# The last stage of a convolution-attention-experts kernel: another fixed order, a drain of GpSimd's queue put elsewhere, bias rows in two loads

## The chip, the cores and the metric

One core of one Trainium2 chip runs the whole kernel in one launch. The metric is the device time of an execution in microseconds. Times below are from the kernel before; start times count from the start of the profiled span.

## What is computed

Eight images of 56 x 56 tokens with 128 channels pass a deformable convolution layer (layer 0), then attention, then an expert layer, all in f32. Only the expert layer matters here:

```python
logits = einsum('bsd,ed->bse', x, gate_w) + gate_b      # x: 8 x 3136 x 128, 64 experts
probs = softmax(logits, axis=1)                          # over the tokens of an image
vals, idx = top_k(probs.transpose(0, 2, 1), 8)           # 8 tokens for each expert and image
pooled = einsum('bked,bke->bed', x[idx], vals)           # one row for each expert and image
h = gelu(concat(pooled, 1) @ weight1)                    # 129 x 512 for each expert
out = concat(h, 1) @ weight2                             # 513 x 128; its last row is the bias
outputs.at[idx].add(out * vals)                          # added to the chosen tokens
```

The result is x + outputs. A token can be chosen by several experts, so an addition in place must not lose any of them.

## The kernel before, in words

Up to some 2540 us the kernel runs convolution, attention and the gate of the experts, interleaved by a list of steps (ORDER) that is fixed in the source. In its last steps it also lays ready the slots: a slot is one of the K = 8 tokens of an expert in an image. `slot_f` holds the slots' token numbers, `slot_c` their weights. What the change touches comes after that: the block `with tc.manual_schedule` at L1974 to L2038, where each engine executes its instructions in the order in which the text writes them, and the call of `store` behind it.

**Names.** The images are in two groups, g = 0 (images 0 to 3) and g = 1 (4 to 7); the 64 experts in two halves, h = 0 and h = 1. So a 128-partition tile holds one group and one half: 4 images x 32 experts. The two layers of the experts are computed in four quarters q of 16 experts: quarters 0 and 1 are half 0, quarters 2 and 3 half 1.

**A quarter.** `hidden(q)` (L1806, 32 matmuls on PE) multiplies by weight1; `unload` copies the result to SBUF (ACT); `turned(q)` transposes it (PE, L1821), adds the bias (DVE, L1822) and applies gelu (ACT, L1827); `outputs(q)` (PE, L1835, 128 small matmuls, then a copy on ACT, L1842) multiplies by weight2; `gathered(q)` transposes (PE, L1847) and files the result in `outT` (DVE, L1849).

**A total.** Several slots can name the same token. For each slot of (g, h), the kernel computes the sum of what all slots of the same token in the same group, in halves h2 <= h, give. `share` (L1584, L1597) builds the weight of expert to slot, in 8 products and 7 additions on DVE for each (g, h, h2); `steps(last, n)` issues n of these pieces. `expand(g, h, h2)` (L1856) spreads such a share over the 4 images into a `wide` tile: for h = 0 with one DVE multiplication (L1860), for h = 1 with four ACT operations (L1870). `totals(g, h, h2)` multiplies `wide` by the experts' outputs `oe` (PE, L1915, 16 matmuls); where h2 = h, it first transposes `outT` (L1906) and adds the bias rows `b2` (DVE, L1909), and at its end adds the sums to the tokens' rows (DVE, L1924, two additions). These rows are in `rows` for g = 0 and `low` for g = 1, gathered from DRAM by POOL's indirect DMAs.

**Repeated slots.** Only one slot of each token may write its row. For g = 1, `first_only(1, h)` marks the others: `again` (DVE, L1883) from `wide` (g, h, h), 16 matmuls in one column each (two passes of 8, L1893, `pc`), `at` and `once` (DVE, L1895 and L1896). A marked slot's row number is put beyond the end, and the store leaves it out.

**The store.** `store(g, h)` (L1953 to L1972) issues 8 indirect DMAs on POOL (L1959), each writing 128 rows of 512 B to the output. The four calls are (0,0), (1,0), (0,1), (1,1). Ahead of half 1 POOL waits for half 0's writes to have landed (`done_`), since rows may be the same tokens; behind (1,0) stands a `drain` of GpSimd (L1972); behind (1,1) a wait for all writes.

**What sets order.** On each engine, the text's order. `gen` is a ring of five PSUM banks that the transposes, `hidden`, `pc` and `pf` share (L282). `freed` hands out SBUF buffers of used weights to `came` (later weight loads on SP), `base`, `expand` and `first_only`, in the order of the calls. SP issues the weight loads (512 KB each) and the loads of `b2` in one queue.

Of the kernel before, what the change touches and what calls it, by code (L numbers as in the profile page):

```python
# [17 lines left out]
C = 128  # L18
# [15 lines left out]
DH = 512  # L34
# [211 lines left out]
def local_kernel(ctx, tc, a, pos, out, flag):  # L246

    nc = tc.nc
# [1485 lines left out]
    w1, w2 = a["L1_ffn_weight1"], a["L1_ffn_weight2"]  # L1734
# [8 lines left out]
    def second_weights(e, pool, tag, bufs):  # L1743

        t = pool.tile([P, EG, 4, C], F32, tag=tag, name=f"w2t{e}", bufs=bufs)
        nc.sync.dma_start(
            t.rearrange("p e f o -> p e (f o)"),
            w2[e : e + EG, :DH, :].rearrange("e (p f) o -> p e (f o)", f=4),
        )
        for k in range(EG):  # L1750
            experts["second", e + k] = t[:, k]
# [50 lines left out]
    def hidden(q):  # L1802
        ph = gen(f"eph{q}")
        for r in range(4):
            for j in range(4):
                nc.tensor.matmul(  # L1806
                    ph[32 * j : 32 * (j + 1), :],
                    pps[q % 2][:, r, j, :],
                    experts["first", EB * q + 4 * r + j],
                    start=r == 0,  # L1810
                    stop=r == 3,
                )
        return ph

    def unload(ph):
        nc.scalar.copy(eh, ph.rearrange("r (h f) -> r f h", f=4))
# [27 lines left out]
    def gathered(q):  # L1844
        pt = gen(f"eot{q}")
        for r in range(4):
            nc.tensor.transpose(pt[:, r * P : (r + 1) * P], eo[:, r, :], ident)  # L1847
        e0 = EB * (q % 2)
        nc.vector.tensor_copy(  # L1849
            outT[:, q // 2, :, e0 : e0 + EB].rearrange("o b e -> o e b"),  # L1850
            pt.rearrange("o (e b) -> o e b", e=EB)[:, :, :NB],
        )
# [3 lines left out]
    def expand(g, h, h2):  # L1856
        pool, tag, n = next(freed)
        wide = pool.tile([P, K, 4, 32], F32, tag=tag, name=f"wide{g}{h}{h2}", bufs=n)
        if h == 0:
            nc.vector.tensor_mul(  # L1860
                wide,
                shares[g, h, h2].unsqueeze(2).to_broadcast([P, K, 4, 32]),
                experts["same"]
                .rearrange("p (b e) -> p b e", b=4)
                .unsqueeze(1)
                .to_broadcast([P, K, 4, 32]),
            )
        else:
            for b in range(4):
                nc.scalar.activation(  # L1870
                    wide[:, :, b],
                    shares[g, h, h2],
                    AF.Copy,
                    scale=experts["same"][:, 32 * b : 32 * b + 1],
                )
        wides[g, h, h2] = wide

    def first_only(g, h):

        pool, tag, n = next(freed)  # L1880
        again = pool.tile([P, K, P], F32, tag=tag, name=f"again{g}{h}", bufs=n)
        wides[g, h] = again
        nc.vector.scalar_tensor_tensor(  # L1883
            again,
            wides[g, h, h].rearrange("p k b e -> p k (b e)"),
            0.0,
            experts["upper"].unsqueeze(1).to_broadcast([P, K, P]),
            op0=ALU.is_gt,
            op1=ALU.mult,
        )  # L1890
        pc = gen(f"pc{g}{h}")
        for k in range(K):
            nc.tensor.matmul(pc[:, k : k + 1], again[:, k], unit, start=True, stop=True)  # L1893
        at = experts["pool"].tile([P, 2, K], F32, tag="twice", name=f"at{g}{h}")[:, 0]
        nc.vector.tensor_scalar_add(at, slot_f[:, g, h], float(4 * g * T))  # L1895
        nc.vector.scalar_tensor_tensor(  # L1896
            experts["once", g, h], pc[:, :K], float(NB * T), at, op0=ALU.mult, op1=ALU.add
        )
# [3 lines left out]
    def totals(g, h, h2):  # L1902

        if h2 == h:
            pt = gen(f"pt_o{g}{h}")
            nc.tensor.transpose(  # L1906
                pt[:, :P], outT[:, h, 4 * g : 4 * g + 4, :].rearrange("o b e -> o (b e)"), ident
            )
            nc.vector.tensor_add(oes[g, h], pt[:, :P], b2[:, h])  # L1909
        for k0 in range(0, K, 4):  # L1910
            if h2 == 0:
                pfs[g, h, k0] = gen(f"pf{g}{h}_{k0}")
            pf = pfs[g, h, k0]
            for k in range(4):
                nc.tensor.matmul(  # L1915
                    pf[:, k * C : (k + 1) * C],
                    wides[g, h, h2][:, k0 + k].rearrange("p b e -> p (b e)"),
                    oes[g, h2],
                    start=h2 == 0 and k == 0,
                    stop=h2 == h and k == 3,  # L1920
                )
            if h2 == h:
                r = rows[g, h][:, k0 : k0 + 4].rearrange("p k c -> p (k c)")
                nc.vector.tensor_add(r, r, pf)  # L1924

    def steps(line, n):

        for _ in range(n):
            got = next(line, None)
            while got is not None and got.when and not got.us:  # L1930
                got = next(line, None)

    def came(which, n):
        load, todo = (first_weights, second_weights)[which], left[which]
        for _ in range(min(n, len(todo))):
            load(todo.pop(0), *next(freed))
# [16 lines left out]
    def store(g, h):  # L1953
        for k0 in range(0, K, 4):
            with tc.tile_critical(no_gpsimd_drain=True):
                if h and not g and not k0:
                    nc.gpsimd.wait_ge(done_, 16 * 2 * K)
                for k in range(k0, k0 + 4):
                    nc.gpsimd.indirect_dma_start(  # L1959
                        out=every,  # L1960
                        out_offset=bass.IndirectOffsetOnAxis(
                            ap=experts["once", g, h][:, k : k + 1], axis=0
                        ),
                        in_=rows[g, h][:, k, :],
                        in_offset=None,
                        bounds_check=NB * T - 1,
                        oob_is_err=False,
                    ).then_inc(done_, 16)
                if h and g and k0:
                    nc.gpsimd.wait_ge(done_, 16 * 4 * K)  # L1970
                elif g and k0:
                    nc.gpsimd.drain()  # L1972

    with tc.manual_schedule(engines=engines):  # L1974
        for k, at in enumerate(first_at):
            first_weights(EFIRST + EG * k, *at)
        for k, at in enumerate(second_at):
            second_weights(EFIRST + EG * k, *at)
        for pp in pps:
            nc.gpsimd.memset(pp.rearrange("p r j e -> p (r j e)"), 0.0)  # L1980
        pos_ = [ps.tile([P, 512], F32, tag=t, name=f"epo_{t}") for t in ("held", "av")]
        for t in pos_:
            nc.vector.memset(t, 0.0)
        widen(0)
        widen(1)
        steps(slots(NB // 2 - 1), 9)
        last = share(1)
        steps(last, 3)
        unload(hidden(0))
        for h in range(2):  # L1990
            for _ in base(1, h):
                pass
        steps(last, 1)
        ph = hidden(1)
        came(0, 9)
        b2 = fin.tile([P, 2, C], F32, tag="b2", name="b2")
        for h in range(2):
            for q in range(4):
                nc.sync.dma_start(b2[32 * q : 32 * q + 32, h], w2[32 * h : 32 * h + 32, DH, :])
        came(0, 2)  # L2000
        widen(2)
        steps(last, 9)
        turned(0)
        unload(ph)
        widen(3)
        steps(last, 6)
        for g in range(2):
            expand(g, 0, 0)
        outputs(0)
        turned(1)  # L2010
        first_only(1, 0)
        came(1, 8)
        gathered(0)
        outputs(1)
        came(1, 4)
        unload(hidden(2))
        steps(last, 15)
        gathered(1)
        for g in range(2):
            totals(g, 0, 0)  # L2020
        turned(2)
        ph = hidden(3)
        unload(ph)
        expand(0, 1, 0)
        expand(1, 1, 0)
        steps(last, 99)
        outputs(2)
        turned(3)
        for g in range(2):
            totals(g, 1, 0)  # L2030
        gathered(2)
        for g in range(2):
            expand(g, 1, 1)
        first_only(1, 1)
        outputs(3)
        gathered(3)
        for g in range(2):
            totals(g, 1, 1)  # L2038
    for h in range(2):
        for g in range(2):  # L2040
            store(g, h)
# [813 lines left out]
```

## Time and profile before

| | |
|---|---|
| median of 3 runs | 2654.75 us (2653.42 to 2655.34) |
| the profiled execution's own time | 2656.84 us |
| its span | 2655.0 us |
| granted TensorE clock, mean | 0.972 |
| busy: PE, DVE, ACT, POOL | 93%, 82%, 73%, 82% |
| the experts' stage | about 2540 to 2626 us, then the stores of half 1 |
| POOL's stores, half 0 | 2595.48 to 2616.39 us, 16 DMAs |
| drain L1972 | 2608.04 to 2623.66 us |
| POOL's stores, half 1 | 2626.60 to 2646.89 us, 16 DMAs |

In the profile, PE is TensorE, PEld its weight loads, DVE VectorE, ACT ScalarE, POOL GpSimd, SP the engine that issues most loads. "POOLq" is POOL's instruction sequencer; it takes drains, waits and moves, and goes ahead of the engine behind it. In a timeline each line has start, duration, engine, source line, operation and operands; the bracket holds the engine's idle time before it and what ended that. In a table of windows each engine's busy time in a stretch stands with its count of instructions, and PEclk is the granted clock.

### The profile page before, as it was taken

The page shows a single profiled execution, that of the slowest core. Times are in us where ns is not written, and L with a number is a line of the kernel's source. Part 1 is how long each engine was busy: PE and PEld are TensorE (multiplying, and loading weights), DVE is VectorE, ACT ScalarE, POOL GpSimd, SP SyncE. Part 2 cuts the span into 40 slices and gives each one's busy share as a digit, 9 for nine tenths or more (in the row PEclk, how much of TensorE's full clock was granted, in tenths as well). Part 3 has the DMA queues.
Part 4 walks back from the last instruction along what each step waited for, and adds up shares of the span by engine and source line. Part 5 has one row for each costly group of instructions (what it writes and reads, how often), then busy time and mean ns, then how long its engine had stood idle before and what let it go on. Part 6 is the DMA issues. An engine that isn't in the chain of part 4 may idle for free. (4 is left out here: it accounts for less than half of the span.)

```text
span 2655.0 us, 47647 instructions
## 1 busy us (share of the span) xinstructions
PE 2472.8 (93%) x16297; PEld 1887.9 (71%) x16297; DVE 2164.0 (82%) x4659; ACT 1948.4 (73%) x4532; POOL 2180.2 (82%) x2315
## 2 busy tenths in 40 slices
PE   3799999999999999999999899999999999999974
PEld 3677877777776778777776667767777777777743
DVE  6888877899898987888889897888889988865662
ACT  2356787888787887888778677977888887876631
POOL 3686889889998899989899899987998899882244
PEclk8799999999999999999999999999999999999987
DMA  5665544544554454545454354544465445325083
GB/s 159 204 214 205 208 163 161 198 128 158 189 190 125 160 194 173 175 150 167 169 183 151 122 198 170 181 149 148 162 201 171 145 166 192 136 88 197 23 276 119
DMA packets 274416, 442.63 MB, mean 167 GB/s; under 512 B 14452, under 2 KB 127476, under 8 KB 274164
## 3 DMA queue, kind: packets, MB, share of 16 engines
q1 hardware_dynamic: 184340, 382.09, 41.4%
q10 hardware_dynamic: 86464, 50.94, 6.3%
q0 software_dynamic: 3360, 6.45, 0.8%
q8 instruction: 132, 2.16, 0.4%
q14 instruction: 120, 0.98, 0.1%
HBM read 386.04 MB, written 53.48 MB: 166 GB/s over the span
## 5 line engine op out<-in xcount | busy, mean ns | idle before, releaser
L732 POOL TENSOR_TENSOR g<-g 128x128 f32<-128x128 f32 (+6 forms) x1075 | 1420.9, 1331 | 105.6 <-DVE g L715 25.4
L715 DVE TENSOR_TENSOR g<-g,tp 128x3200 f32<-128x3200 f32 (+1 forms) x200 | 695.0, 3477 | 18.3 <-ACT tp L706 15.9
L1203 PEld LDWEIGHTS av<-v,pe 128*128 128x128 f32 (+2 forms) x5200 | 627.6, 188 | 97.3 <-issue 60.9
L1203 PE MATMUL av<-v,pe 128*128 128x129 f32 (+2 forms) x5200 | 682.7, 277 | 2.8 <-ACT pe L1173 1.6
L1066 PE MATMUL sc<-zT,qT 128*128 128x384 f32 (+8 forms) x1622 | 656.9, 516 | 17.1 <-DVE S L1092 9.9
L1092 DVE TENSOR_SCALAR_CACHE_REDUCE S<-sc 128x512 f32<-128x512 f32 (+5 forms) x783 | 443.3, 576 | 210.1 <-PE sc L1066 124.7
L1140 ACT ACTIVATE S<-S,low 128x512 f32<-128x512 f32 (+5 forms) x783 | 478.8, 638 | 41.9 <-DVE low L1108 30.1
L1173 ACT COPY pe<-tr 128x512 f32<-128x512 f32 (+3 forms) x775 | 380.2, 501 | 144.2 <-PE tr L1158 110.5
L1158 PE MATMUL tr<-ident,S 128*128 128x128 f32 x2516 | 392.3, 276 | 12.6 <-DVE S L1092 9.5
L1158 PEld LDWEIGHTS tr<-ident,S 128*128 128x128 f32 x2516 | 297.0, 142 | 130.7 <-issue 67.0
L1066 PEld LDWEIGHTS sc<-zT,qT 128*128 128x128 f32 (+1 forms) x1622 | 246.6, 187 | 114.1 <-issue 43.3
L576 DVE SCALAR_TENSOR_TENSOR pv<-xg,dw,pv 128x448 f32<-128x448 f32 x448 | 305.7, 682 | 14.2 <-ACT pv L573 8.4
L877 PEld LDWEIGHTS pm<-fc,hid 128*128 128x128 f32 x1600 | 200.4, 193 | 37.6 <-issue 22.6
L877 PE MATMUL pm<-fc,hid 128*128 128x128 f32 x1600 | 222.2, 282 | 1.8 <-POOL hid L862 1.3
L856 PE MATMUL ph<-xT,fc 128*128 128x512 f32 (+2 forms) x448 | 207.3, 551 | 5.2 <-DVE xT L803 3.2
L863 ACT ACTIVATE hid<-ph,b_fc 128x512 f32<-128x512 f32 (+2 forms) x224 | 140.8, 634 | 95.8 <-PE ph L856 92.8
L667 POOL TENSOR_TENSOR taps<-taps,a 128x252 f32<-128x252 f32 (+1 forms) x288 | 191.9, 666 | 8.8
L657 POOL TENSOR_TENSOR a<-w 128x756 f32<-128x756 f32 (+1 forms) x96 | 136.5, 1422 | 20.9 <-DVE w L648 18.4
L760 ACT COPY ys<-ptg 128x128 f32<-128x128 f32 (+1 forms) x200 | 52.6, 263 | 89.4 <-PE ptg L749 47.5
L1140 ACT ACT_TABLE_LOAD x87 | 111.6, 1283 | 4.6 <-DVE pv L576 2.3
L749 PE MATMUL ptg<-ident,g 128*128 128x128 f32 (+1 forms) x650 | 92.0, 307 | 21.7 <-POOL g L732 21.6
L749 PEld LDWEIGHTS ptg<-ident,g 128*128 128x128 f32 (+1 forms) x650 | 88.6, 221 | 25.5 <-POOL g L732 23.7
(328 smaller groups left out, 3712.8 us busy)
## 6 DMA issues: line engine op xcount, KB each, us to landing
g<-img SPq DMA_DIRECT2D x192, 1600.0 KB
w1t<-in_L_ffn_weight_dram SPq DMA_DIRECT2D x32, 512.0 KB
w2t<-in_L_ffn_weight_dram SPq DMA_DIRECT2D x32, 512.0 KB
xin<-in_x_dram SPq DMA_DIRECT2D x56, 224.0 KB
xTd<-xc ACTq DMA_DIRECT2D x56, 224.0 KB
img<-st ACTq DMA_DIRECT2D x112, 112.0 KB
out_dram<-t ACTq DMA_DIRECT2D x24, 448.0 KB
g<-img SPq DMA_DIRECT2D x8, 800.0 KB
```

What stands on the lines that cost most here:

```text
L576: nc.vector.scalar_tensor_tensor(p3, src, dw[:, k : k + 1], p3, op0=ALU.mult, op1=ALU.add)
L667: nc.gpsimd.tensor_add(dst, dst, a5[:, :nt, kx])
L715: nc.vector.tensor_mul(g3, g3, tp[:n, lt % 4].unsqueeze(2).to_broadcast([n, NTAP * NG, 32]))
L732: nc.gpsimd.tensor_add(g[:n, o * C : (o + w) * C], g[:n, o * C : (o + w) * C], g[:n, i * C : (i + w) * C])
L856: nc.tensor.matmul(ph[:, :n], fc1[:, f * P : (f + 1) * P], xT[:, :n], start=True, stop=True)
L877: nc.tensor.matmul(four(pm, m)[:, i, :], h[:, i * P : (i + 1) * P], fc2[:, f, :], start=False, stop=i == m - 1 and f == 3,)
L1066: nc.tensor.matmul(pp[h * HALF : h * HALF + qw, c0 : c0 + m], qT[:, q0 : q0 + qw], zTs[b, g][:, k0 : k0 + m], start=True, stop=not seg.las ...
L1092: nc.vector.tensor_scalar(S[p0:p1, c0:c1], pp[p0:p1, c0:c1], -SCALE, None, ALU.mult, ALU.min, accum_out=(mn[p0:p1, i, j + k : j + k + 1] i ...
L1140: nc.scalar.activation(S[p0:p1, c0:c1], S[p0:p1, c0:c1], AF.Exp, bias=low[p0:p1, i : i + 1], scale=-1.0)
L1158: nc.tensor.transpose(pt[:m, k + p0 : k + w], S[p0:w, k : k + m], ident[p0:w, p0:w])
L1173: nc.scalar.copy(pe[:, : full * P], pt[:, : full * P])
L1203: nc.tensor.matmul(p3[h * HALF : h * HALF + qw, i % 3, :], pe[:kw, k + h * HALF : k + h * HALF + qw], vs[b, g][:kw, (k0 + k - c0) // P, :] ...
```

## The change

It consists of four edits in the experts' stage.

- `expand` uses DVE where h == h2 (before: where h == 0), so the wide tiles of (0,1,1) and (1,1,1) are made by DVE and no longer by ACT.
- The drain leaves `store` and is written behind the first loads of the manual block, ahead of the memsets of `pp`.
- `b2` is loaded by two DMAs with a broadcast source of four copies, instead of eight of 32 partitions each.
- The order: `expand(1,0,0)` behind `turned(1)`; `first_only(1,0)` behind `totals(1,0,0)`; `totals(0,0,0)` ahead of `unload(hidden(2))` and `totals(1,0,0)` after it; the 15 steps of one share split into 11 ahead of `gathered(1)` and 4 behind `unload(ph)` of quarter 3; the last steps behind the totals of h2 = 0; `first_only(1,1)` at the very end.

```diff
@@ expand
-        if h == 0:
+        if h == h2:
             nc.vector.tensor_mul(
@@ store
                 if h and g and k0:
                     nc.gpsimd.wait_ge(done_, 16 * 4 * K)
-                elif g and k0:
-                    nc.gpsimd.drain()
@@ the manual block
         for k, at in enumerate(second_at):
             second_weights(EFIRST + EG * k, *at)
+        nc.gpsimd.drain()
         for pp in pps:
@@
         for h in range(2):
-            for q in range(4):
-                nc.sync.dma_start(b2[32 * q : 32 * q + 32, h], w2[32 * h : 32 * h + 32, DH, :])
+            nc.sync.dma_start(
+                b2[:, h], w2[32 * h : 32 * h + 32, DH, :].unsqueeze(0).to_broadcast([4, 32, C])
+            )
@@
         steps(last, 6)
-        for g in range(2):
-            expand(g, 0, 0)
+        expand(0, 0, 0)
         outputs(0)
         turned(1)
-        first_only(1, 0)
+        expand(1, 0, 0)
         came(1, 8)
         gathered(0)
         outputs(1)
         came(1, 4)
+        steps(last, 11)
+        gathered(1)
+        totals(0, 0, 0)
         unload(hidden(2))
-        steps(last, 15)
-        gathered(1)
-        for g in range(2):
-            totals(g, 0, 0)
+        totals(1, 0, 0)
+        first_only(1, 0)
         turned(2)
         ph = hidden(3)
         unload(ph)
-        expand(0, 1, 0)
-        expand(1, 1, 0)
-        steps(last, 99)
+        steps(last, 4)
+        for g in range(2):
+            expand(g, 1, 0)
         outputs(2)
         turned(3)
         for g in range(2):
             totals(g, 1, 0)
+        steps(last, 99)
         gathered(2)
-        for g in range(2):
-            expand(g, 1, 1)
-        first_only(1, 1)
+        expand(0, 1, 1)
         outputs(3)
         gathered(3)
-        for g in range(2):
-            totals(g, 1, 1)
+        totals(0, 1, 1)
+        expand(1, 1, 1)
+        totals(1, 1, 1)
+        first_only(1, 1)
```

## The prediction

> **What bounds the kernel now.** Page first: PE is busy 93% of 2655.0 us, so anything that is cut ahead of the experts' stage would count. But the diff touches only the last 115 us, so I went to that stage's windows, then to the chain that ended last, then to the timelines of POOL, PE and DVE from 2540 us on. The windows show that PE's bound is over there:
>
> ```profile
> core 0: us, PE busy (x) PEld busy (x) DVE busy (x) ACT busy (x) POOL busy (x), PEclk, DMA share, GB/s
> ...
> 2595.00:2610.00 15.00, 12.80 (x211) 9.76 (x209) 10.82 (x21) 8.72 (x20) 11.17 (x12) 1.00 0.71 259
> 2610.00:2626.00 16.00, 12.98 (x176) 11.06 (x177) 2.87 (x8) 0.59 (x1) 5.17 (x5) 0.79 0.08 27
> 2626.00:2655.00 29.00, 0.91 (x9) 0.72 (x7) 1.37 (x2) 0.00 (x0) 15.72 (x16) 0.58 0.11 37
> ```
>
> For the last 29 us only POOL works. The chain of waits is POOL's scatters (L1959) and their issue, nothing else:
>
> ```profile
> by line: POOL out_dram L1959 0.3%; issue 0.2%; POOLq L2850 0.0%; POOLq L1959 0.0%
> ```
>
> So the end is: the first scatter of half 1, fifteen more behind it, and a tail. POOL's timeline (start, duration, operation, idle before) gives the places:
>
> ```profile
> 2595.48 1.02 POOL L1959 DMA_INDIRECT out_dram<-rows,once  x1 [13.27 <-PE pf L1915]
> ...
> 2615.41 0.98 POOL L1959 DMA_INDIRECT out_dram<-low,once  x1 [0.30 <-issue]
> 2626.60 0.98 POOL L1959 DMA_INDIRECT out_dram<-rows,once  x1 [10.21 <-PE pf L1915]
> ...
> 2645.91 0.98 POOL L1959 DMA_INDIRECT out_dram<-low,once  x1 [0.30 <-issue]
> ```
>
> Sixteen scatters take 16 x 1.287 = 20.3 us (2626.60 to 2646.89); from there to the end of the span are 8.1 us. Two things come before the one at 2626.60. The rows it stores get their last addition (L1924) from 2623.92 to 2624.61, 1.99 us ahead of it (store(0,0): 2593.40 to 2595.48, 2.08). And the drain of L1972:
>
> ```profile
> L1972 POOLq DRAIN  x1: 15622/15622/15622, 2608.0 to 2608.0; - x1
> ```
>
> It ends at 2608.04 + 15.62 = 2623.66, 0.95 us ahead of that addition. So the addition ends last; an earlier addition alone would gain 0.95 us and then meet the drain.
>
> **Part 1: the order, and wide of half 1 on DVE.** Five rows of PE (start, duration, operation, idle before) show what marking the repeated slots costs where it stands now:
>
> ```profile
> 2577.79 1.92 PE L1893 MATMUL pc<-unit,again 128*128 128x1 f32 x16 [2.15 <-DVE at L1895]
> 2579.57 1.02 PE L1847 MATMUL eot<-ident,eo 128*128 128x128 f32 x4
> 2580.51 4.91 PE L1835 MATMUL epo_av<-w2t,hb 128*8 128x128 f32 x128
> ...
> 2610.53 3.55 PE L1893 MATMUL pc<-unit,again 128*128 128x1 f32 x16 [2.73 <-DVE at L1895]
> 2614.01 5.22 PE L1835 MATMUL epo_av<-w2t,hb 128*8 128x128 f32 x128
> ```
>
> PE stood 2.15 us ahead of the first pc and 2.73 us ahead of the second, and outputs after each took 4.91 and 5.22 us where outputs(2) took 3.68: the granted clock is 0.50 in 2579.67 to 2583.09 and in 2610.39 to 2617.22. After the change the first pc stands behind the totals, the second behind everything. I walked the new order with before's durations; the start of an instruction is the later of its engine being free and its input being there:
>
> - *Half 0.* hb(1) stays at 2575.83 (eht1 ends 2575.64); as outputs(0) began 1.40 us after its hb, outputs(1) begins at 2577.2 (before 2580.51) and at 3.6 us ends at 2580.8; copy 0.59, eot1 until 2582.0. DVE meanwhile has the second wide (1.17), outT0 (0.37) and 11 share steps (15 took 7.7, so 5.7), until 2583.2; outT1 until 2583.6. In before, outT1 ended at 2589.85 and the last addition to rows of (0,0) at 2593.40, 3.55 later: now 2587.15. First scatter 2.08 behind it: **2589.2** (before 2595.48).
> - *Between.* hidden(2) follows pf00 on PE, 2586.15 to 2589.6; then pf of (1,0) from 2590.3, its rows done at 2593.1 (2.78 from pf's start to the second addition's end, as in before: 2590.62 to 2593.40); again (1.21) until 2594.3, pc 1.8 until 2596.0, eht2 2596.5, hidden(3) until 2600.0, outputs(2) until 2603.6. Before had these two at 2596.07 and 2599.53: the gain of half 0 is spent here, because pc and its 1.9 us of idle PE come into this stretch, and hidden(3) starts as late as ever.
> - *Half 1.* eht3 2604.1; hb(3) 2604.9, gelu 2605.6; the two pf of h2 = 0 until 2607.7 and eot2 until 2608.3. No pc follows, so outputs(3) runs 2608.2 to 2611.8 (before 2614.01 to 2619.2), eot3 from 2612.9. Now DVE is the later one: 15 steps (7.7) from 2604.9 until 2612.6, outT2 (0.3 more), wide011 (1.17, new on DVE) until 2614.0, outT3 2614.4. In before, outT3's end was at 2621.06 and rows(0,1) were done at 2624.61, 3.55 later: now 2617.9. First scatter 1.99 behind: **2619.9** instead of 2626.60, **-6.7 us**.
>
> The scatters of half 0 end at 2589.2 + 16 x 1.30 = 2610.1 and cover nothing. Clock: a new idle of 1.9 us stands ahead of pc(1,0). The window 2575.86 to 2579.27, with PE busy 1.48 of 3.41 us, was followed by half clock; 2617.22 to 2620.63, with 2.64, was not. The new gap's window holds about 2.4: nearer the second. A half-clock window costs up to 1.7 us; I take 0 and keep 1.7. (The Trainium skill, "TensorE: Matmul & The Clock Gate", Part 1, gives a free-running window of 3.4 us and half clock after an idle one, with no idle over some 3.4 us as the working rule. The window's length agrees with the rows, the working rule does not: 2.15 us sufficed. By the rule the new gap costs nothing; by the row it may cost 1.7.)
>
> Moving wide(1,1,1) from ACT (4 x 0.41) to DVE costs 1.17 us twice in all on DVE; one is counted above, the other stands ahead of pf11. This gives the order's own debt: rows(0,1) 2617.9, wide111 2619.1, pf11, low(1) 2622.2, again 2623.4, pc(1,1) 1.9 to 3.55, once at **2625.7 to 2627.4**. store(1,1) is due at 2619.9 + 8 x 1.287 = 2630.2, and needs its values some 2.0 earlier, 2628.2. It fits by 0.8 to 2.5 us: cost 0, else up to 2.
>
> **Part 2: bias in two loads.** Eight loads on SP at 1.7 us each become two; SP's w1t and w2t loads behind them move up by some 4 us (last landing 2604 to about 2600). hidden(3) at 2596 and outputs(3) at 2608 come later than their weights in both. b2 lands around 2582.5, needed for oe00 at 2584: cost 0. If it lands later, half 0 is late by as much, up to 1 us, and by "Between" half 1 too.
>
> **Part 3: the drain.** In the changed program the drain isn't where the text puts it: it carries no dependency, and in POOL's instruction list it stands right behind the six constant loads and the memset of xg (L495), some 7.5 us into the span, 2500 us ahead of this stage. There its next users come 8 us later: cost 0. What it used to do is then left to the drain at the program's end, which now stands behind 98 DMAs of POOL (104 less six) where it stood behind 16. The price of that is read from three drains:
>
> ```profile
> L2850 POOLq DRAIN  x3: 46/109/1364, 2652.7 to 2654.6; - x3
> ```
>
> The longest here is the end's: 1.36 us, with 16 DMAs behind the drain of L1972, all landed. The drain of L1972 had 88 DMAs; the last landed at 2617.64, and it ended 6.02 us later. One at the start, with no DMA ahead, took 0.31. A line through the first and last of these, 0.31 + 0.0656 per DMA, gives 6.08 for 88: it hits the third within 1%. For 98 it gives 6.74: **+5.4 us**. Counted from POOL's last scatter instead (2616.39, 7.27 us for 88, 0.083 each) it is 8.1: +6.7. The other end: what L1972 waited for is a fixed time after the last DMA (7.27 there, 2646.89 to 2654.04 = 7.15 at the end: these agree as well!); then the end costs 0. I take +5.4, since the third point was not used for the line.
>
> **Sum.** -6.7 + 0 + 0 + 5.4 = -1.3 us against the profiled execution's 2656.84 (span 2655.0 and 1.84 around it): 2655.5. The timed runs have their median 2.1 below that execution, at 2654.75; against it the sum is 2653.5. A measurement of this kernel tells about 0.2%, 5.3 us, from no change: the forecast is **no change**, with its own range of 2652 to 2657 (clock +1.7, drain +1.3, bias and store up to 1).
>
> **Rivals.**
>
> 1. *The end's drain is free (faster).* If the 7.2 us are a fixed time after the last DMA, the order's gain stays: -6.7, or -5 with one half-clock window: 2648 to 2650. For it: the two intervals agree within 2%. Against: at the end all had landed 4.5 us before the drain began, so little of a fixed latency could be left in it, and yet it took 1.36.
> 2. *POOL runs out of room (slower).* No drain stands between the first scatter and the last, so up to 98 DMAs go unreclaimed, ten more than any row of before shows. If issuing waits past a limit between 88 and 98, POOL stalls among its last ten scatters, on the chain itself, for about one reclaiming, 6.0 us (2617.64 to 2623.66): -1.3 + 6.0 = +4.7, with the dearer drain +6: 2658 to 2661. It decides once a stall is over 4 us. [...] Against: the 88th was issued at the same 1.29 us as the first.
> 3. *The order doesn't give 6.7.* Half clock in hidden(3) and outputs(2) (2 windows, 3.4), and store(1,1) late by 2: -1.3, and the drain's +5.4 to 6.7: +4 to +5.4, 2659 to 2660. Against: PE has little idle, see the window above.
> 4. *More than the walk.* If DVE's steps overlap better, or SP's earlier loads matter, and the drain costs under 4: 2646 to 2649.
>
> **Chances.** Forecast 0.46; drain free 0.25 (most of it over 0.2%: 0.20); room 0.13 (0.10 over); order 0.10 (0.06 over), more than the walk 0.06. Faster by over 0.2%: 0.26 with rival 4, and 0.04 for a walk that errs along with a cheap drain, 0.30; slower 0.20 with 0.04 for a drain dearer than its line; same 0.50. The range takes in the free drain and the room's stall: 2646 to 2661.
>
> **What would show it.** Right: the first half-0 scatter at 2589, the first half-1 scatter at 2620, sixteen at 1.287 behind it, no L1972 row, the end's drain 6.7 us long. Wrong: that drain at about 1.4 (rival 1), a gap over 0.3 us between two of the last ten scatters (rival 2), PEclk of 0.5 in 2597 to 2604 or a gap ahead of the 9th scatter of half 1 (rival 3).

## The result and the profile after

The changed kernel takes 2662.43 us (median of 7 runs, 2660.49 to 2664.88), the kernel before 2653.83 us (7 runs): a ratio of 1.0032, 95% interval 1.0020 to 1.0044. It is slower by about 8.6 us, outside the forecast's range. The profiled execution took 2662.82 us with a span of 2660.7, 6.0 and 5.7 us over the one of before.

POOL's timeline of the changed kernel, first and last scatter of each half (start, duration, operation, idle before):

```profile
2589.29 1.02 POOL L1959 DMA_INDIRECT out_dram<-rows,once  x1 [9.80 <-DMA w2t<-in_L_ffn_weight_dram]
...
2608.65 0.98 POOL L1959 DMA_INDIRECT out_dram<-low,once  x1 [0.30 <-issue]
2623.84 0.98 POOL L1959 DMA_INDIRECT out_dram<-rows,once  x1 [14.21 <-DVE oe L1909]
...
2643.64 0.98 POOL L1959 DMA_INDIRECT out_dram<-low,once  x1 [0.30 <-issue]
```

The last scatter starts 2.3 us earlier than in before, and yet the span ends 5.7 us later. What lies behind it is on POOL's sequencer. The lines are those of three source lines in the changed kernel, and then one of before (minimum, median and maximum of a group in ns, then the start of its first and its last in us):

```profile
L1977 POOLq DRAIN  x1: 1510/1510/1510, 6.7 to 6.7; - x1
```

```profile
L2804 POOLq INC_SWDGE_SEM  x1: 1843/1843/1843, 2649.9 to 2649.9; - x1
```

```profile
L2851 POOLq DRAIN  x3: 46/109/8072, 2651.7 to 2660.4; - x3
```

```profile
L2803 POOLq INC_SWDGE_SEM  x1: 363/363/363, 2652.3 to 2652.3; - x1
```

The moved drain ran 6.7 us into the span, more than 2500 us ahead of the stage, as the forecast read from the program. The end's drain took 8.07 us instead of 1.36, INC_SWDGE_SEM 1.84 instead of 0.36. From the last scatter's end to the end of the span are 16.1 us instead of 8.1.

A ledger of the 5.7 us, with outputs(0)'s start as the mark, since nothing that the diff orders anew binds ahead of it:

| stretch | before | after | change | forecast |
|---|---|---|---|---|
| span's start to outputs(0) | 2571.37 | 2569.86 | -1.5 | 0 |
| outputs(0) to half 1's first scatter | 55.23 | 53.98 | -1.25 | -6.7 |
| its 16 scatters | 20.29 | 20.78 | +0.5 | 0 |
| last scatter to the end | 8.11 | 16.08 | +8.0 | +5.4 |

The first row is a difference between executions as far as the profile shows. The third is one scatter of 1.49 us in the place of 0.98; it runs beside DVE's `again` (2627.11 to 2628.33), which the new order put there. This row does come with the new order: the sixteen take 20.3 us in all three traces with the order of before, and 20.5 to 22.8 us in all seventeen with the new one. Why the scatter is longer wasn't tested. Two rows are larger: a tail that grew by 8.0, and an order that gave 1.2 in the place of 6.7.

For the second, PE's timeline of the changed kernel:

```profile
2582.13 0.41 PE L1906 MATMUL pt_o<-ident,outT 128*128 128x128 f32 x1 [1.39 <-DVE outT L1849]
2582.92 3.34 PE L1915 MATMUL pf<-oe,wide 128*128 128x128 f32 x16 [0.38 <-DVE oe L1909]
...
2594.61 2.37 PE L1893 MATMUL pc<-unit,again 128*128 128x1 f32 x16 [2.08 <-DVE at L1895]
2596.84 1.09 PE L1821 MATMUL eht<-ident,eh 128*128 128x128 f32 x4
2597.86 6.03 PE L1806 MATMUL eph<-w1t,pp 128*32 128x512 f32 x32
2603.72 3.67 PE L1835 MATMUL epo_held<-w2t,hb 128*8 128x128 f32 x128
```

The first pf takes 3.34 us where 2.05 is its time at full clock, hidden(3) 6.03 in the place of 3.64. The windows around them (PE's busy time is the second number, PEclk the third from the right):

```profile
2578.80:2582.20 3.40, 1.25 (x25) 0.73 (x16) 3.10 (x7) 0.58 (x1) 0.69 (x1) 1.00 1.05 381
2582.20:2585.60 3.40, 3.02 (x13) 2.75 (x14) 0.86 (x2) 0.00 (x0) 0.00 (x0) 0.51 1.05 389
2592.40:2595.85 3.45, 1.37 (x14) 1.27 (x12) 1.98 (x3) 0.00 (x0) 2.54 (x4) 1.00 1.05 390
2595.85:2599.30 3.45, 3.45 (x19) 2.08 (x22) 1.39 (x4) 0.54 (x1) 2.84 (x3) 0.51 0.83 311
2599.30:2602.70 3.40, 3.40 (x20) 0.79 (x16) 1.31 (x3) 0.10 (x1) 2.49 (x4) 0.50 0.21 74
```

Twice a window in which PE was busy for less than 1.4 of 3.4 us is followed by half clock, once for one window, once for two. Outputs(2) starts 33.9 us after outputs(0); the forecast had 28.6. So 5.2 of the missing 5.5 us were gone by then.

### The profile page after: what moved, and what is told of

The parts are those of the page before. It is cut to its first block, busy times and chain, and to the rows that moved or that the text cites. A ratio compares the mean times of both kernels' runs of the same rounds, so it can differ in the third digit from the quotient of the medians.

```text
span 2660.7 us, 47636 instructions
## 1 busy us (share of the span) xinstructions
PE 2467.7 (93%) x16297; PEld 1881.9 (71%) x16297; DVE 2169.0 (82%) x4661; ACT 1943.7 (73%) x4524; POOL 2178.3 (82%) x2315
## 5 line engine op out<-in xcount | busy, mean ns | idle before, releaser
L657 POOL TENSOR_TENSOR a<-w 128x756 f32<-128x756 f32 (+1 forms) x96 | 136.5, 1422 | 20.6 <-DVE w L648 18.1
L760 ACT COPY ys<-ptg 128x128 f32<-128x128 f32 (+1 forms) x200 | 52.5, 262 | 90.3 <-PE ptg L749 47.1
```

## The experiments

The theory to test has two parts. **A:** a drain costs 0.05 us and 0.082 for each of POOL's DMAs since the last drain, wherever it stands, and the change moves that work from a covered place to the end. **D:** the new order is 5 to 6 us shorter, but leaves PE idle, and loses most of that to half clock. The rivals: **B**, the new order itself is slower and the drain only fills a time that is there anyway; **E**, another thing (DVE, the weights) sets half 1; **F**, the drain has a fixed cost or a threshold.

The runs were made in five sets, each with its own runs of the kernel before. In two sets outputs(0) starts at 2587 to 2599 us and outputs(2) comes in pieces ("late sets", where before takes 2700.2 and 2698.9 us); in the other three outputs(0) starts near 2570, as in the first profile ("early sets": 2654.8, 2654.8 and 2656.5). Both late sets ran on one chip, the early sets on three others. The expectations below put the late start down to weights that land late. The traces don't show that: in all eight late ones, DVE's bias addition ahead of outputs(0) waits 13.6 to 14.6 us for something that no record names, and in the kernel with the drain put back the last packet of the queue that carries the weights ends at 2612.18, 16 us ahead of outputs(2). What holds PE there stays open. Ratios are to the runs of before of the same set. A distance "from outputs(0)" is from that PE group's start to half 1's first scatter in the profile; it is 55.2 us in before and 54.0 in the changed kernel.

**The drain alone: put back, and moved alone.**

```diff
 drain_back, against the changed kernel:
-        nc.gpsimd.drain()                  # in the manual block
...
                     nc.gpsimd.wait_ge(done_, 16 * 4 * K)
+                elif g and k0:
+                    nc.gpsimd.drain()      # in store
 drain_only: the reverse, against the kernel before
```

> The changed kernel with the drain back in store, behind half 0's scatters. Theory A (a drain costs about 0.083 us for each POOL DMA since the last one, wherever it stands; INC_SWDGE_SEM at the end grows likewise): the drain at the end takes 1.4 us again instead of 8.07, INC_SWDGE_SEM 0.36 instead of 1.84, from the last scatter's end to the span's end 8.1 us instead of 16.1; the drain in the middle takes 7.3 us from the last half-0 scatter's end, until about 2617, ahead of half 1's rows, so it holds nothing up. Time 8 us under the changed kernel: 2654, about the kernel before or 1 to 2 us under it. Rival B (the new order itself is slower, the drain only shows more of an idle time that is there anyway): 2660 or more.

> The kernel before with only the drain moved as in the change. Theory A: the first half-1 scatter stays where it was (half 1's rows ended last there), the end's drain takes 8.1 us and INC_SWDGE_SEM 1.8: 8 us over the kernel before, 2662. Rival B (the order is slower): within 2 us of the kernel before.

This was a late set. Drain put back: 2692.20, ratio 0.9971 (0.9959 to 0.9983). Drain moved alone: 2706.95, ratio 1.0026 (1.0015 to 1.0037). B falls: the order alone isn't slower, the drain alone is. The drain in the middle ended 7.26 us behind half 0's last scatter and 13.4 us ahead of half 1's first; the drains at the end took 1.36 and 8.07 us. The order's gain of 8 us in this set was more than expected of it.

To have them beside the changed kernel itself, in an early set:

> The changed kernel once more, so that it stands beside the others in one set of runs. Theory A with what the runs so far show (the order gains some 8 us where the drain is put back, the moved drain costs 7 to 8): about the time of the kernel before, if this set's loads are as slow as in the set before; 5 to 8 us over the kernel before, if the weights land early as in the first profile.

> The changed kernel with the drain back in store, a second time, beside the changed kernel itself. Theory A: 8.2 us under the changed kernel (6.7 of the end's drain, 1.5 of INC_SWDGE_SEM), wherever the stage starts. Rival: another difference, since these two were never in one set.

Changed kernel: 2664.17, ratio 1.0032 (1.0021 to 1.0043). Drain put back: 2654.95, ratio 0.9998 (0.9989 to 1.0007), 9.2 us less where 8.2 were expected. The changed kernel's second trace is like its first: the clock falls twice (at 2581.4 and 2598.5), outputs(2) starts 33.8 us and half 1 53.9 us behind outputs(0). And the drain alone in another early set:

> The kernel before with only the drain moved, a second time. Theory A: 8.2 us over the kernel before with early weights too (6.7 in the end's drain, 1.5 in INC_SWDGE_SEM), less up to 1 if the middle drain had held the first half-1 scatter. Rival: the drain's move costs less where half 1 isn't waiting for weights, under 5.

2663.28, ratio 1.0030 (1.0019 to 1.0041), 8.5 us over the kernel before. The two kernels' drains at the end, drain put back first:

```profile
L2852 POOLq DRAIN  x3: 46/109/1364, 2648.2 to 2650.1; - x3
```

```profile
L2849 POOLq DRAIN  x3: 46/109/8072, 2651.2 to 2659.8; - x3
```

The change's whole loss is the moved drain: with the order of before it costs as much as with the new one, and the new order with the drain put back is level with before in an early set.

**The price for each DMA.** Two more places:

```diff
 drain_72:
-        nc.gpsimd.drain()                  # in the manual block
...
+    with tc.tile_critical(no_gpsimd_drain=True):
+        nc.gpsimd.drain()
     for h in range(2):
         for g in range(2):
             store(g, h)
 drain_first: instead, in store behind its waits
+                if not (h or g or k0):
+                    nc.gpsimd.drain()
                 for k in range(k0, k0 + 4):
```

> The changed kernel with the drain in a section of its own between the manual block and the stores, in POOL's idle time ahead of the first scatter: 72 DMAs before it, 32 behind it. Theory A: 72 x 0.082 + 0.05 = 6.0 us in the middle, 32 x 0.082 + 0.05 = 2.7 at the end, INC_SWDGE_SEM 0.65: the end 1.6 us longer than with the drain put back, 6.6 shorter than in the changed kernel. Rival F (the end's drain is long only past some number of DMAs, or lasts a fixed time): 1.4 or 8.1 at the end.

> The changed kernel with the drain inside the first store, behind its waits and ahead of its first scatter: 72 DMAs before it, 32 behind it (the drain in a section of its own ran at 15 us, behind 6 DMAs, and left 98 to the end's). Theory A, 0.05 + 0.0818 for each DMA: 5.9 us here, 2.7 at the end, INC_SWDGE_SEM 0.65; half 0's scatters start 6 us later and still end ahead of half 1's rows; 6.5 us under the changed kernel, 1.6 over the one with the drain put back. Rival F (a threshold or a fixed time): 1.4 or 8 at the end.

drain_72 missed its purpose: with nothing to hold it, the drain ran at 15.1 us, behind the six constant loads alone, and the kernel is the changed one again (2663.35, ratio 1.0030, 1.0020 to 1.0041). It gives a point all the same, its first line here, then the end's:

```profile
L2040 POOLq DRAIN  x1: 551/551/551, 15.1 to 15.1; - x1
```

```profile
L2852 POOLq DRAIN  x3: 46/109/8066, 2652.8 to 2661.4; - x3
```

drain_first (late set) was held by store's waits:

```profile
L1959 POOLq DRAIN  x1: 5952/5952/5952, 2619.5 to 2619.5; - x1
```

```profile
L2852 POOLq DRAIN  x3: 46/109/2667, 2697.8 to 2701.1; - x3
```

So, for drains that begin when POOL's DMAs have been issued: 6 DMAs 0.55 us, 16 1.36, 32 2.67, 72 5.95, 98 8.07. A line 0.06 + 0.0818 n meets all five within 0.011 us. Drains that begin while POOL is still at work fit it when counted from the end of that work: the middle drain of before and of the drain put back, with 88 DMAs, 7.27 and 7.26 us from the last scatter's end (the line gives 7.26), and the moved drain, with 6, 0.59 of its 1.51 us from a memset's end at 7.65. F falls, and A stands. INC_SWDGE_SEM took 0.36, 0.51 and 1.84 with 16, 32 and 98: it grows too, but not on a line. The kernel itself was level with before in its late set (2698.43, 0.9997, 0.9987 to 1.0006), where the drain put back gained 8 in another: half 0's scatters start later by the drain, and the end is 1.3 us longer. That isn't the 1.6 us alone that was expected; the sets differ, so how much of the rest is the place isn't told.

**The other parts.** The order alone, and another split of the share pieces, both with the drain put back and in the late set:

```diff
 order_only:
-        if h == h2:
+        if h == 0:
...
+            for q in range(4):
+                nc.sync.dma_start(b2[32 * q : 32 * q + 32, h], w2[32 * h : 32 * h + 32, DH, :])
 steps_7_4:
-        steps(last, 11)
+        steps(last, 7)
         gathered(1)
         totals(0, 0, 0)
+        steps(last, 4)
```

> The changed kernel with three parts undone: drain in store, eight bias loads, the wide tiles of half 1 on ACT; only the order is new. Theory C (bias loads and wide tiles are off the path): within 1.5 us of the kernel with the drain put back (2654), since ACT is idle where the tiles are made. Rival: the 8 loads delay half 0's first total by over 1 us, or the wide on ACT takes away the 1.17 us that DVE spends ahead of the last outT copy: 1 to 3 us either way.

> As the kernel with the drain put back, but 7 of the 11 share pieces ahead of gathered(1) and 4 behind totals(0,0,0), so that outT(1) doesn't wait behind DVE's pieces. Theory D (PE's clock fell in the window in which PE stood idle for outT(1), and again ahead of pc; the new order lost some 5 us to it): PE's idle ahead of the first pt_o shrinks from 1.4 to under 0.6 us, no half clock in the first pf (2.05 us instead of 3.34), hidden(2) 2 to 3 us earlier, the first half-1 scatter 2 to 3 us earlier than with the drain put back: 2651 to 2652, or less if the second half-clock stretch goes too. Rival E (the end of half 1 is set by DVE's 15 pieces, whatever the clock): no gain, 2654.

2691.59 (0.9966, 0.9954 to 0.9978) and 2693.75 (0.9975, 0.9965 to 0.9986), beside 2692.20 with the drain put back. The bias loads and the place of the wide tiles can't be told from nothing in this set, as forecast. The split can't be judged here: in this set outputs(2) comes in pieces, so that what is gained ahead of it need not reach the end. PE's timeline of the kernel with the drain put back ("issue": the profile shows nothing that was waited for):

```profile
2628.61 1.70 PE L1835 MATMUL epo_held<-w2t,hb 128*8 128x128 f32 x42
2630.66 0.38 PE L1835 MATMUL epo_held<-w2t,hb 128*8 128x128 f32 x3 [0.35 <-issue]
2631.44 0.29 PE L1835 MATMUL epo_held<-w2t,hb 128*8 128x128 f32 x2 [0.40 <-issue]
```

From the end of outputs(2) to half 1's first scatter are 21.2 us with before's order (the drain moved alone) and 16.5 with the new one. What follows outputs(2) is shorter by 4.7: the second marking no longer stands there, whose pc took 1.92 us behind a wait of 2.06 in the trace with before's order. That is the larger part of the 8 us; the rest wasn't followed up.

**The clock.** PE's idle stretches filled with throwaway transposes of ident, which the next instruction overwrites (they add work and change no value):

```diff
+    def keep_busy(t, n):
+        for _ in range(n):
+            nc.tensor.matmul(t[:, :P], ident, ident, start=True, stop=True)
...
         pc = gen(f"pc{g}{h}")
+        keep_busy(pc, 17 if h == 0 else 0)      # warm; 8 in warm_fit
```

and the same ahead of eot(1) (5; then 2), ahead of the first pt_o (12; then 6), and in warm_fit ahead of eot(3) (4).

> As the kernel with the drain put back, with 34 throwaway transposes of ident by PE, into tiles that the next instruction overwrites: 5 ahead of eot(1), 12 ahead of the first pt_o, 17 ahead of the first pc, to fill PE's idle time there. Theory D (the half clock of these stretches took some 5 us of the order's gain): clock 1.0 from outputs(1) to hidden(3), hidden(3) 3.6 us instead of 6.0, first half-1 scatter 3 to 5 us earlier. Rival E (DVE or the weights set half 1): no earlier than with the drain put back.

> As the kernel with 34 throwaway transposes, but with their number cut to the idle time (each took 0.23 us at full clock, not the 0.11 that their number was taken from): 2 ahead of eot(1), 6 ahead of the first pt_o, 8 ahead of the first pc, and 4 ahead of eot(3). Theory D: full clock as there, and outputs(2) about 2 us sooner after outputs(0): first half-1 scatter 50 us behind outputs(0)'s start (before 55.2, drain put back 52.5, 34 transposes 52.2), time 4 to 5 us under the kernel before. Rival E (something else sets half 1): 52 us again.

> The fitted throwaway transposes, a second time. Where outputs(0) starts near 2570 (weights early), theory D: no half clock from 2562 to 2615, first half-1 scatter 50 us behind outputs(0)'s start, 4 to 5 us under the kernel before; rival E: 52 us, 1 to 2 under. Where it starts near 2595 the run doesn't tell.

warm, early set: 2653.08, ratio 0.9992 (0.9983 to 1.0001). The clock is 1.0 from 2559 to 2624 us, hidden(3) takes 3.64 us (the profiled execution is the fastest of the eleven): with the stretches filled, the half clock doesn't come. But half 1 is 52.2 us from outputs(0), as good as with the drain put back (52.5): a transpose took 0.23 us where 0.11 was reckoned, so the 17 ahead of pc lasted 3.8 us in a gap of 2.1 and gave back what the clock gained. warm_fit in a late set (2692.57, 0.9969, 0.9957 to 0.9981) doesn't tell. In an early set it took 2652.48 (0.9993, 0.9984 to 1.0002), 51.7 us from outputs(0): here half clock came once more, from 2596.3 to 2599.7, over hidden(3) (5.3 us), although PE had stood still for only 0.20 us ahead of pc. PE's timeline (a transpose has two records), and the window that ends where the clock falls:

```profile
2591.77 1.95 PE L1804 MATMUL pc<-ident 128*128 128x128 f32 x16
2593.91 1.95 PE L1899 MATMUL pc<-unit,again 128*128 128x1 f32 x16 [0.20 <-DVE again L1888]
2595.72 0.63 PE L1825 MATMUL eht<-ident,eh 128*128 128x128 f32 x4
2596.28 5.33 PE L1810 MATMUL eph<-w1t,pp 128*32 128x512 f32 x32
```

```profile
2592.92:2596.33 3.41, 3.21 (x32) 2.85 (x33) 1.19 (x3) 0.00 (x0) 2.63 (x3) 1.00 1.05 394
```

PE was busy for 3.21 of 3.41 us there, so idle time alone isn't the cause. 1.95 us of it are pc's matmuls of one column each. In each of the 20 traces the clock changes only at points that lie 3.41 us or a multiple of it apart. Of the windows between such points, 34 at full clock hold more than 0.3 us of pc: the 23 with at most 1.41 us of other PE work were followed by half clock, the 11 with 1.87 us or more kept the full one. So pc counted like idle time. This is a reading of the traces; no run tests it by itself.

**pc out of PE's way.** The marking cut in two: again (DVE) where it is, pc's matmuls behind hidden(3).

```diff
 in first_only, behind again:
+        yield
...
         totals(1, 0, 0)
-        first_only(1, 0)
+        only = first_only(1, 0)
+        next(only)              # again
         turned(2)
         ph = hidden(3)
+        next(only, None)        # pc, at, once
         unload(ph)
```

> The changed kernel with the drain back in store and with the first marking's pc matmuls behind hidden(3) on PE, again as before ahead of turned(2). Theory D: PE no longer stands 2.1 us ahead of pc, the clock is full in hidden(3) (3.6 us), which starts some 4 us sooner; store(1,0) may wait up to 1 us for once. First half-1 scatter 48 to 50 us behind outputs(0)'s start if the first half-clock stretch doesn't come, 50 to 51 if it does: 3 to 5 us under the kernel before. Rival E: 52 us, no gain over the drain put back.

> pc of the first marking behind hidden(3), a second time, no throwaway work. Weights early, theory D: 48 to 51 us from outputs(0) to the first half-1 scatter, 3 to 5 us under the kernel before; rival E: 52, 1 to 2 under.

Late set: 2693.47 (0.9976, 0.9966 to 0.9986), no better than the drain put back in another late set. Early set: 2652.70 (0.9991, 0.9982 to 1.0000), 49.5 us from outputs(0), full clock from 2560 to 2611 in the profiled execution (again the fastest of the eleven), with no throwaway work. That is 3.0 us nearer than with the drain put back, so E falls in this trace; the median is 2.1 us under before, less than the 3 to 5 expected. store(1,0) waited 1.2 us for once.

**All of it.** The kernel with pc behind hidden(3), and besides with the pieces split 7 and 4, eight more pieces of the last share ahead of turned(3), and 8 transposes (2 ahead of eot(1), 2 ahead of the first pt_o, 4 ahead of eot(3)).

> The last kernel with 7 and 4 share pieces around totals(0,0,0), 8 pieces of the last share ahead of turned(3), and 8 throwaway transposes (2 ahead of eot(1), 2 ahead of the first pt_o, 4 ahead of eot(3)). Theory D: no half clock before 2620, rows of half 1 some 6 us sooner than with the drain put back; then the drain in the middle binds (half 0's scatters end 20.8 us behind their first, drain 7.3, 2 to the first scatter): 30 us from half 0's first scatter to half 1's, 48 from outputs(0)'s start; time 6 to 7 us under the kernel before. Rival: no more than the other.

> pc behind hidden(3), share pieces spread, 8 throwaway transposes, a second time. Weights early, theory D: the middle drain binds, 48 us from outputs(0) to the first half-1 scatter, 6 to 7 us under the kernel before; rival E: 51 to 52, at most 2 under.

Late set: 2687.24, ratio 0.9943 (0.9929 to 0.9957), with runs from 2682.1 to 2692.6. Early set: **2649.48, ratio 0.9979 (0.9970 to 0.9988)**, 5.3 us under before, and by the ratios (0.9979 against 1.0032) some 14 under the changed kernel: it beats both. It is 48.5 us from outputs(0). PE in its profile:

```profile
2587.74 2.05 PE L1922 MATMUL pf<-oe,wide 128*128 128x128 f32 x16 [0.38 <-DVE oe L1916]
2589.63 0.60 PE L1825 MATMUL eht<-ident,eh 128*128 128x128 f32 x4
2590.16 3.64 PE L1810 MATMUL eph<-w1t,pp 128*32 128x512 f32 x32
2593.73 1.95 PE L1899 MATMUL pc<-unit,again 128*128 128x1 f32 x16
2595.60 3.68 PE L1839 MATMUL epo_held<-w2t,hb 128*8 128x128 f32 x128
```

No idle stands ahead of pc, hidden(3) runs at full clock, and outputs(2) starts 26.2 us after outputs(0) instead of 33.9. The windows of this kernel, and then of the one with the drain put back, at the same times:

```profile
2585.00:2595.00 10.00, 9.62 (x85) 4.99 (x77) 4.80 (x9) 2.29 (x5) 6.48 (x6) 1.00 1.05 389
2595.00:2605.00 10.00, 10.00 (x219) 9.60 (x222) 8.79 (x20) 3.92 (x9) 7.40 (x9) 1.00 0.47 165
```

```profile
2585.00:2595.00 10.00, 7.54 (x69) 4.93 (x62) 3.18 (x7) 0.58 (x1) 6.09 (x7) 0.98 1.05 389
2595.00:2605.00 10.00, 10.00 (x174) 5.71 (x167) 3.33 (x7) 4.95 (x12) 7.80 (x8) 0.85 0.40 145
```

PE is busy 9.6 us of the first ten here and 7.5 there, and does 219 against 174 matmuls in the second.

Half 1's rows were done by 2613.0 (pf's start and 2.78), but its first scatter came at 2617.90: half 0's scatters end at 2608.29, the middle drain 7.27 later at 2615.56, and the scatter 2.3 behind. So now the drain binds. A last pair, in an early set, tries a drain ahead of half 0's scatters, held there by a copy of one column:

```diff
+    seen = fin.tile([P, 1], F32, tag="seen", name="seen")
+    with tc.tile_critical(no_gpsimd_drain=True):
+        nc.gpsimd.tensor_copy(seen, wides[0, 0, 0][:, 0, 0, :1])
+        nc.gpsimd.drain()
     for h in range(2):
...
-                elif g and k0:
-                    nc.gpsimd.drain()
```

> As the kernel with pc behind hidden(3), spread pieces and 8 throwaway transposes, with the drain between the gathers of low and the first scatter, held there by a small copy on POOL from wide(0,0,0), and none behind half 0's scatters. If the middle drain binds: 6.0 us of drain in POOL's idle time, half 0's scatters no later, half 1's first scatter 2 to 3 us sooner; the end 1.5 us longer (32 DMAs: 2.7 and 0.5): 0.5 to 1.5 us under the other. If half 1's rows bind too: no sooner, and 1.5 us over it.

> The same kernel with the drain behind half 0's scatters, beside it: 5 us under the kernel before where the weights land early (9 to 12 where they land late).

2649.78 (0.9976, 0.9967 to 0.9985) and 2649.19 (0.9972, 0.9963 to 0.9981): level. The copy waited 6.3 us on POOL, the drain ran from 2588.88 to 2595.04, and half 0's scatters began 25.0 us behind outputs(0) instead of 17.8. They ended at 2618.80, and half 1's first followed 2.05 us later: half 0 bound in the drain's place. Half 1 starts 0.7 us sooner by the profiles (47.9 against 48.6), and the end is 1.25 us longer.

## Why the prediction was wrong, by its own steps

Three steps failed: the half clock was priced at nothing, the drain's term was too small, and INC_SWDGE_SEM had no term. Rival 3, with half clock and the dearer drain, came nearest (2659 to 2660).

- **"Half 0."** Right in its instants up to the first total: outputs(1) 5.8 us behind outputs(0) (forecast 5.8), the first pt_o 12.3 (forecast 12.2). But the step didn't look at its own idle: from outputs(1)'s end PE has 0.8 and 1.4 us without work, the window's busy time is 1.25, and the first pf ran at half clock (+1.3). That the first scatter came at 2589.29, as forecast, is luck: counted from outputs(0) it came 1.6 us late, and the stage began 1.5 us early.
- **"Clock: ... I take 0 and keep 1.7."** This failed, and it is the larger error in the order. The window for which it expected "about 2.4" held 1.37. Its own walk has pc from 2594.3 to 2596.0, so most of that 2.4 was pc itself, which by the traces didn't hold the clock. The row that it compared with was also read 0.4 us too early: before's clock fell at 2579.68, and in the 3.41 us ahead of that PE was busy for 1.89, all of them pc. So 2.15 us of waiting was not the whole of what "sufficed" there. The price was for one window; three came, some 4.6 us by the rows: pf +1.3, pc +0.5, eht +0.4, hidden(3) +2.4. Rival 3 had this mechanism, with two windows and 3.4 us, and was given 0.10; its late store(1,1) didn't come. That PE's work in these stretches decides is shown by the traces of warm (full clock, hidden(3) 3.64) and of the kernels with pc behind hidden(3).
- **"Between."** Wrong by what the clock took: outputs(2) came 33.9 us behind outputs(0) instead of 28.6.
- **"Half 1."** Right: forecast 19.9 us from outputs(2)'s start to half 1's first scatter, measured 20.1; also in warm (20.1). In the best kernel the drain holds it at 22.3.
- **"The order's own debt."** once(1,1) was ready at 2630.8, 3.8 us ahead of store(1,1)'s first scatter: no wait, as forecast. But its `again` now runs beside the scatters, and one of them is 0.5 us longer.
- **Parts 1 and 2, wide tiles and bias.** Nothing that can be measured, as forecast; tested in a late set only.
- **"For 98 it gives 6.74: +5.4 us."** The mechanism was right, the term too small: 8.07, so +6.7. The line's first point was misread. In the trace of before, the drain at the start begins at 0.31 us and takes 0.18, most of it beside memsets that run until 0.45; the line of the runs gives 0.06 with no DMA. The reading that was set aside, counted from POOL's last scatter (8.1), was the right one: it gives 1.32 for the end's 1.36. That the line met its third point "within 1%" was chance.
- **The term that was left out:** INC_SWDGE_SEM stood in the tail at 0.36 us and grew to 1.84, +1.5. Only the drain was priced, though its neighbour on the sequencer had a duration in the same place.
- **Rivals 1 and 2.** The end's drain isn't free, and no scatter among the last ten stalled: 98 DMAs went without a drain at 1.29 us each, but for one of 1.79, the fourth of half 1. The kernels with the drain put back have such a longer one too.
- **A slip that changes nothing:** 16 x 1.287 is 20.6; the 20.3 us of the trace are fifteen steps of 1.287 and one scatter of 0.98.

By the measured terms the sum would have been -1.2 + 0.5 + 6.7 + 1.5 = +7.5, against a median that moved by 8.6, and by 9.4 in the second set. With a full clock it would have been about +2.0.

What stays partly open: the kernel with the drain put back has a first half-1 scatter 2.7 us sooner than before in the one profiled execution of an early set, but its median is level with before (2654.95 and 2654.81). 0.7 us of the 2.7 go again in the sixteen scatters (21.0 and 20.3 us). The granted clock of its eleven runs differs too: four, the profiled one among them, had 0.978 to 0.980 and took 2652.2 to 2652.5 us, seven had 0.970 to 0.974 and took 2653.6 to 2657.7. Before has both kinds as well, with medians of 2653.9 and 2655.7. Like against like, the new order is then some 1.5 and 0.4 us ahead. Why not the 2.0 that the trace leaves, isn't shown.

## What to carry to other kernels

Work that an engine puts off until a drain has a price for each item, and it is paid at the next drain: before one is moved, count what stands behind every later one, the program's last among them, and check in the instruction list where it ends up. A walk of a new order with the old order's durations is good to half a microsecond as long as the clock is the same; where it leaves PE idle for two microseconds and more, or with matmuls of one column only, take the half clock as likely and price it for several windows. Small matmuls that wait for another engine are better put behind large ones than ahead of them: in the one profiled execution this alone kept the full clock without added work.

## What the runs showed of the hardware that was not expected

- A drain of GpSimd's queue takes 0.06 + 0.0818 us for each DMA issued since the last one, from 6 to 98 DMAs, long after they have landed: at the end of the changed kernel the last one landed at 2645.89 and the drain began at 2651.74.
- No window with PE busy for less than 1.44 of 3.41 us kept the full clock, in any of the 20 traces; a wait of 2.0 us was enough for it (changed kernel, ahead of the last pf: 1.41 us busy, half clock from 2623.2). The Trainium skill, "TensorE: Matmul & The Clock Gate", Part 1, gives the same window of some 3.4 us, and as its working rule no idle over some 3.4 us; the rule was too lenient here.
- Matmuls of one column did not hold the clock: in the kernel with fitted transposes it fell after 3.21 us of PE work, 1.95 of them pc.
- After such a fall the clock stayed at half through a window in which PE was busy for all of 3.45 us, with pc, the transposes and the begin of hidden(3), and through the next.
- The same kernel before takes 2655 to 2657 us in three sets and 2699 to 2700 in two, which ran on another chip; in the traces of those two outputs(0) starts at 2587 to 2599 us instead of 2568 to 2573. The distance between two kernels changes with it (the drain put back: level, and 8 us faster).
